# Column copies on VectorE, zeros from ScalarE, and one scaled table a step in a fused transformer and state-space kernel

## The chip, the cores and the metric

The kernel runs as one program on one core of a Trainium2 chip. The metric is the time on the device in microseconds (us), the median of three runs. TensorE is called PE here, VectorE DVE, ScalarE ACT, GpSimd POOL, and SyncE, which issues all the DMAs, SP. "L390" is line 390 of the kernel before.

## What is computed

The input is x, 2048 tokens of 128 features, and everything is in float32. The reference does three things in a row:

```
x = x + 0.5 * ffn(layernorm(x))
x = x + mamba(layernorm(x))
x = x + 0.5 * ffn(layernorm(x))          # the same weights again

def ffn(x):                              # 6 layers
    for i in range(6):
        x = attn_layer(shift_tokens(x), ...) + x
        x = ff_layer(shift_tokens(x), ...) + x
    return x

def shift_tokens(t):                     # the second half of the features is moved by one token
    a, s = split(t, 2, -1)
    return concatenate([a, pad(s, one token in front)[:, :-1]], -1)
```

An attention layer has 16 heads of 64 features. Queries and keys are normalised to length one, multiplied by learned scales and rotated with tables of cosines and sines that depend on the token (`q * cos * scale + rotate_half(q) * sin * scale`). Attention is local: each window of 32 tokens looks at itself and at the window before it; before the first window there is nothing. A feed-forward layer is a layer normalisation, a matmul to twice 341 features, a product of one half with the gelu of the other, and a matmul back. `mamba` is a selective state-space layer with 256 inner features and 16 states, a scan over all 2048 tokens.

## The kernel before

**Tiles and stages.** Features lie on the partitions, tokens in the columns. The 2048 tokens are two segments of 1024 (`SEG`), each eight tiles of 128 (`ST` = 8). The work on one tile in one layer is cut into some 50 stages. A stream of 192 tiles runs through them: the first pass takes segment 0 through its six layers, then segment 1 through its six, and the second pass (`again`) does the same once more. So tile `g` has a segment, a layer and a place `t` from 0 to 7, and 24 stretches of eight tiles follow each other. Stages that work on 256 tokens (the feed-forward ones, and the loading of tables) run once for two tiles, a pair.

**Order.** Nothing is left to a scheduler on PE, DVE, ACT and POOL: the table `ORDER` gives each stage a lag in tiles and a position within a step. In step `i`, `run` calls the stages in the order of their positions, each for tile `i - lag`, and every engine works through its own instructions in that order. So work of up to eight tiles is in flight. Work that belongs to no tile (merging weights, the state-space layer between the passes, the loading of tables for a pair) is put among the stages with `at_time(step + position, ...)`. The order of the DMAs on SP is chosen by the framework from the same program; each is issued when what it waits for is done, and those behind it wait.

**The parts that the change touches.**

The shift by one token is made by storing: a result's second half of partitions is written one column further to the right (`halves`). The residual streams `r0` (one for each segment) and `r1` therefore have 1025 columns, and column 0 of partitions 64 to 127 is what came before the segment: zero for segment 0, and for segment 1 the last column of segment 0 in the same layer. Those last columns are kept in `c0` and `c1`, one column a layer. POOL copies them: L377 and L784 put the last column of `r0` into `c0` (L784 after the feed-forward residual L772 of the pair that ends segment 0), L655 puts that of `r1` into `c1`. POOL also puts them back: L1205 copies `c0` into column 0 of `r0` just before the first projection (`project`, L390) of a layer in segment 1, and L647 copies `c1` into `r1`. In segment 0, L649 sets that column of `r1` to zero on POOL. The state-space layer writes `r0` anew between the passes (`entered`, L375).

Keys and inputs of the window before a tile come from the tile before it (L494, L599). At the head of segment 0 there are none, and POOL writes zeros: L502 into 256 columns of the keys `kt`, L603 into 32 partitions of the inputs `xw`.

The rotation uses tables of cosines and sines multiplied by the layer's learned scales. `tables(p)` makes them for pair `p`. In segment 0 of the first pass it loads the plain table (L292), POOL multiplies it by the scales (L293), it is used, and it is also saved in DRAM for the second pass (L296). At the same place the table of the tokens 1024 further on, which segment 1 will need, is loaded, multiplied and saved. Later, tables are loaded ready (L302). `tables` is called at the stage `TB`, position 0.898 of every odd step, for the next pair; for the first pair it is called at time -1.95, after all weights that the start needs have been issued by `begin`.

On the way of one tile, the lines that the following sections name are: project (L390, two for queries and keys), sines and cosines on DVE (L416, L409), squares on ACT (L402), their sum on DVE (L432), the rotation's addition on POOL (L426), a floor under the sums on POOL (L439), roots on ACT (L444), the copy of the inputs on ACT (L593), the scaling on POOL (L458), scores, maxima, subtraction on POOL (L553), exponent on ACT (L559), divisors on DVE (L564, L565), division on POOL (L569), the average over the window on PE (z_ps, L614), its copy on ACT (L626), mixing by merged value and output weights on PE (L635), the residual on DVE (L651). Merged weights are made at the start (L249, L256) and stored in DRAM (L258).

Of the kernel before, what the change touches and what calls it, by code (L numbers as in the profile page):

```python
# [9 lines left out]
F32 = mybir.dt.float32  # L10
# [7 lines left out]
P = 128  # L18
N = 2048
NB = N // 512  # L20
DEPTH = 6
# [3 lines left out]
WIN = 32  # L25
# [31 lines left out]
ST = 8  # L57
SEG = ST * P
# [59 lines left out]
def halves(at, n):  # L118


    return tuple((rows, bass.ds(at + shift, n)) for rows, shift in SIDES)


class Stream:
# [158 lines left out]
    def tables(self, p):  # L283


        nc, k, st = self.nc, self.k, self.at[2 * p]
        flat = "p a b d -> p (a b d)"

        def scaled(tok, tag, bufs):
            tab = self.sb.tile([P, 4, 2, DH], F32, tag=tag, name="tab", bufs=bufs)  # L290
            at = tok // P % 4
            nc.sync.dma_start(out=tab, in_=k.tabs[:, tok // 512, :, at : at + 2, :])  # L292
            nc.gpsimd.tensor_tensor(  # L293
                tab, tab, st.w.sc.unsqueeze(2).to_broadcast([P, 4, 2, DH]), ALU.mult
            )
            nc.sync.dma_start(out=k.scaled_tabs[st.layer][tok // SUB], in_=tab.rearrange(flat))  # L296
            return tab

        if st.again or st.seg:
            self.tabs[p] = self.sb.tile([P, 4, 2, DH], F32, tag="tab", name="tab")  # L300
            saved = k.scaled_tabs[st.layer][st.tok // SUB]
            nc.sync.dma_start(out=self.tabs[p].rearrange(flat), in_=saved)  # L302
        else:
            self.tabs[p] = scaled(st.tok, "tab", 2)
            scaled(st.tok + SEG, "tab2", 1)

    def next_tables(self, f):
        if f + 1 < len(self.ff):
# [64 lines left out]
    def entered(self, seg, col, xc, q):  # L373
        for rows, cols in halves(col, SUB):
            self.nc.gpsimd.tensor_tensor(self.r0[seg][rows, cols], xc[rows], q[rows], ALU.mult)  # L375
        if seg == 0 and col + SUB == SEG:
            self.nc.gpsimd.tensor_copy(self.c0[64:, 0:1], self.r0[0][64:, SEG : SEG + 1])  # L377

# [108 lines left out]
    def keys_before(self, g):  # L489


        nc, k, st = self.nc, self.k, self.at[g]
        if st.t:
            nc.scalar.activation(  # L494
                st.kt[:, :, 0:WIN], self.at[g - 1].kt[:, :, P:], AF.Identity, scale=k.ratio
            )
        elif st.seg:
            last = self.sb.tile([P, 8, WIN], F32, tag="last", name="last", bufs=1)
            nc.sync.dma_start(out=last.rearrange("p c k -> p (c k)"), in_=k.last_keys[st.layer])
            nc.scalar.copy(st.kt[:, :, 0:WIN], last)  # L500
        else:
            nc.gpsimd.memset(st.kt[:, :, 0:WIN], 0.0)  # L502
        if st.seg == 0 and st.t == ST - 1:
            last = self.sb.tile([P, 8, WIN], F32, tag="last", name="last", bufs=1)
            nc.scalar.activation(last, st.kt[:, :, P:], AF.Identity, scale=k.ratio)
            nc.sync.dma_start(out=k.last_keys[st.layer], in_=last.rearrange("p c k -> p (c k)"))
# [88 lines left out]
    def inputs_before(self, g):  # L595
        nc, k, st = self.nc, self.k, self.at[g]
        nc.sync.dma_start(out=st.xw[WIN:, 0], in_=st.xw[0 : P - WIN, 1])
        if st.t:
            nc.sync.dma_start(out=st.xw[0:WIN, 0], in_=self.at[g - 1].xw[P - WIN :, 1])  # L599
        elif st.seg:  # L600
            nc.sync.dma_start(out=st.xw[0:WIN, 0], in_=k.last_inputs[st.layer])
        else:
            nc.gpsimd.memset(st.xw[0:WIN, 0], 0.0)  # L603
        if st.seg == 0 and st.t == ST - 1:
            nc.sync.dma_start(out=k.last_inputs[st.layer], in_=st.xw[P - WIN :, 1])

# [36 lines left out]
    def residual(self, g):  # L643
        nc, st = self.nc, self.at[g]
        if st.t == 0:
            if st.seg:
                nc.gpsimd.tensor_copy(self.r1[64:, 0:1], self.c1[64:, st.layer : st.layer + 1])  # L647
            else:
                nc.gpsimd.memset(self.r1[64:, 0:1], 0.0)  # L649
        for rows, cols in halves(st.t * P, P):  # L650
            nc.vector.tensor_tensor(  # L651
                self.r1[rows, cols], st.y_ps[rows, :], self.r0[st.seg][rows, cols], ALU.add
            )
        if st.seg == 0 and st.t == ST - 1:
            nc.gpsimd.tensor_copy(  # L655
                self.c1[64:, st.layer : st.layer + 1], self.r1[64:, SEG : SEG + 1]
            )

# [107 lines left out]
    def ff_residual(self, f):  # L766

        nc, st, o = self.nc, self.first(f), self.ff[f].o_ps
        i = V_B2 + st.layer
        for rows, cols in halves(st.t * P, SUB):  # L770
            done = st.layer == DEPTH - 1
            nc.vector.scalar_tensor_tensor(  # L772
                o[rows] if done else self.r0[st.seg][rows, cols],
                o[rows],
                self.k.pv[rows, i : i + 1],
                self.r1[rows, cols],
                ALU.add,
                ALU.add,
            )
            if done:  # L780
                x = self.x[rows, bass.ds(st.tok, SUB)]
                nc.vector.scalar_tensor_tensor(x, o[rows], 0.5, x, ALU.mult, ALU.add)
        if st.seg == 0 and st.t == ST - 2 and st.layer < DEPTH - 1:
            nc.gpsimd.tensor_copy(  # L784
                self.c0[64:, st.layer + 1 : st.layer + 2], self.r0[0][64:, SEG : SEG + 1]
            )

# [343 lines left out]
    def begin(self, x, tp):  # L1131

        nc, k = self.nc, self.k
        self.tp, self.vo = tp, {}
        xi = tp.tile([P, N // P, P], F32, tag="xi", name="xi")

        def read(b):
            nc.sync.dma_start(
                out=xi[:, 4 * b : 4 * b + 4, :],
                in_=x[bass.ts(b, 512), :].rearrange("(t p) d -> p t d", p=P),  # L1140
            )

        def turn(b):
            t_ps = self.bank2(("t_ps", b), 1)[:, 0]
            for j in range(4):
                nc.tensor.transpose(t_ps[:, bass.ts(j, P)], xi[:, 4 * b + j, :], k.ident)
            nc.scalar.copy(self.x[:, bass.ts(b, 512)], t_ps)
            self.used("t_ps", b)

        activation_tables(nc, EXP_LN)  # L1150
        read(0)
        self.load(0)
        read(1)
        self.load_vo(0)
        self.load_ff(0)
        self.load_vo(1)
        read(2)
        read(3)
        for r in (*self.r0, self.r1):
            nc.gpsimd.memset(r[64:, 0:1], 0.0)  # L1160
        at = self.at_time
        at(-2.0, turn, 0)
        at(-1.95, self.tables, 0)
        time = self.enter(0, -1.9, self.sb)
        at(-1.0, turn, 1)
        for s in range(1, 4):
            time = self.enter(s, max(time + 0.1, 2 * s - 2.9), self.sb)
        at(6.5, turn, 2)
        at(8.5, turn, 3)
        for layer in range(DEPTH):  # L1170
            at(layer + 0.6, self.merge, layer)
            if layer == 0:
                at(0.65, self.load_m, 0)
            if layer + 2 < DEPTH:
                at(layer + 0.7, self.load_vo, layer + 2)
            at(self.room(8 * layer + 3.0, 0.1), self.biases, layer)
        for u in range(1, 2 * UNITS):
            at(8 * u - 6.9, self.load, u)
            at(8 * u - 2.9, self.load_m, u)
            at(8 * u - 0.6, self.load_ff, u)  # L1180
# [17 lines left out]
    def stage(self, i, name, lag):  # L1198
        g = i - lag
        if not 0 <= g < TILES:  # L1200
            return
        elif name in self.TILE:
            if name == "PQ" and g % ST == 0 and self.at[g].seg:
                layer = self.at[g].layer
                self.nc.gpsimd.tensor_copy(self.r0[1][64:, 0:1], self.c0[64:, layer : layer + 1])  # L1205
            method, *args = self.TILE[name]
            getattr(self, method)(g, *args)
        elif g % 2:
            getattr(self, self.PAIR[name])(g // 2)
            if name == "YR" and self.at[g].again and self.at[g].layer == DEPTH - 1:  # L1210
                self.at_time(self.room(i + 1.1, 0.1), self.result, g // 2)
# [3 lines left out]
def macaron_kernel(  # L1215
# [18 lines left out]
    nc = tc.nc  # L1234
    k = Ctx()
# [5 lines left out]
    const = ctx.enter_context(tc.tile_pool(name="const", bufs=1))  # L1241
# [23 lines left out]
    nc.vector.memset(k.eps, LN_EPS)  # L1265
    k.minus_one = const.tile([P, 1], F32, tag="minus_one", name="minus_one")
    nc.vector.memset(k.minus_one, -1.0)
    xt = const.tile([P, N], F32, tag="xt", name="xt")

    dram = ctx.enter_context(tc.tile_pool(name="dram", bufs=1, space=bass.MemoryType.DRAM))  # L1270
# [120 lines left out]
```

## Time and profile before

| | |
|---|---|
| median of 3 runs | 3393.36 us (3391.44 to 3393.8) |
| profiled execution | 3395.29 us, span 3393.5 us |
| granted PE clock, mean | 0.993 |
| PE busy (matmuls) | 3231.5 us, 95% |
| DVE busy | 2797.4 us, 82% |
| ACT busy | 2550.1 us, 75% |
| POOL busy | 2925.4 us, 86% |
| DMA | 181.28 MB, mean 53 GB/s |

The span is what the profiler saw from the first instruction to the last; the execution's own time is 1.8 us longer. Busy time is summed over instructions; waiting, branching and the issuing of DMAs are not counted. A matmul's end is modelled, so that a busy PE need not be at its peak. In a row of the timeline the first number is the start, the second the time, then the engine, the line, the operation, what is written and read (out<-in), the shape, and in brackets how long the engine was idle before it and what ended this.

The lines that the change moves are short: a column copy on POOL takes 183 to 188 ns, the memset of `kt` 305 to 333 ns, of `xw` 195 to 197, of `r1` 99 to 100. A multiply of a table (L293) takes 1262 to 1301 ns, and there are 48.

### The profile page before, as it was taken

To read this page: it belongs to the slowest core of one execution; us is meant where nothing else is said; L and a number is where in the kernel's file an instruction comes from. 1 tells how busy PE (TensorE), PEld (TensorE's weight loads), DVE (VectorE), ACT (ScalarE), POOL (GpSimd) and SP (SyncE) were. 2 spreads that over 40 slices of the span, in tenths; PEclk is the share of its full clock that TensorE was granted. 3 is DMA by queue.
4 is the path that set the end of the run, shared out by engine and by line. 5 is a ranking of instruction groups with operands and counts; after the bars stand their busy time and mean duration, and the time that the engine had idled before them with its cause. 6 is when DMAs were issued, how large, how long until landed. Compare 5 with 4: busy or idle time off the path is not lost. (4 is left out here: it accounts for less than half of the span.)

```text
span 3393.5 us, 97541 instructions
## 1 busy us (share of the span) xinstructions
PE 3231.5 (95%) x41936; PEld 2232.1 (66%) x41936; DVE 2797.4 (82%) x3483; ACT 2550.1 (75%) x4097; POOL 2925.4 (86%) x2397
## 2 busy tenths in 40 slices
PE   5999999999999999999999999999999999999997
PEld 3666666666666666666666666666666676777775
DVE  4777788788888898988989888888888788888884
ACT  4777777777778778787787777877877677777775
POOL 5989899898888988889889898888888888888883
PEclk9999999999999999999999999999999999999999
DMA  7211212111112121111111112112121110111000
GB/s 241 93 62 49 74 54 65 65 61 43 57 44 64 38 55 51 52 49 51 55 39 56 49 44 63 45 44 55 46 55 38 49 33 29 46 36 41 19 12 9
DMA packets 134496, 181.28 MB, mean 53 GB/s; under 512 B 13176, under 2 KB 91312, under 8 KB 127152
## 3 DMA queue, kind: packets, MB, share of 16 engines
q1 hardware_dynamic: 134064, 175.04, 17.4%
q8 instruction: 330, 5.41, 0.7%
q14 instruction: 102, 0.84, 0.1%
HBM read 138.75 MB, written 24.05 MB: 48 GB/s over the span
## 5 line engine op out<-in xcount | busy, mean ns | idle before, releaser
L426 POOL TENSOR_TENSOR rot<-rot,t 128x1024 f32<-128x1024 f32 x384 | 900.8, 2368 | 8.9 <-DVE t L416 4.5
L390 PE MATMUL x_ps<-qk,r 128*128 128x512 f32 x1536 | 756.1, 615 | 27.3 <-ACT zt L626 10.3
L635 PEld LDWEIGHTS y_ps<-zt,m 128*128 128x128 f32 x6144 | 715.3, 192 | 62.0 <-ACT xc L681 30.6
L458 POOL TENSOR_TENSOR rot<-rot,rn 128x1024 f32<-128x1024 f32 x384 | 722.9, 1904 | 14.4
L635 PE MATMUL y_ps<-zt,m 128*128 128x128 f32 x6144 | 718.5, 275 | 3.9 <-ACT xc L681 2.7
L416 DVE TENSOR_TENSOR t<-x_ps,tab 128x1024 f32<-128x1024 f32 x384 | 467.9, 1218 | 161.6 <-PE i_ps L586 86.9
L402 ACT ACTIVATE sq<-x_ps 128x1024 f32<-128x1024 f32 x384 | 393.7, 1025 | 261.1 <-DVE rot L409 212.5
L390 PEld LDWEIGHTS x_ps<-qk,r 128*128 128x128 f32 x1536 | 272.4, 191 | 361.9 <-issue 233.3
L569 POOL TENSOR_TENSOR pr<-pr,rs 128x1024 f32<-128x1024 f32 x192 | 365.4, 1903 | 165.1 <-DVE rs L565 139.9
L409 DVE TENSOR_TENSOR rot<-x_ps,tab 128x1024 f32<-128x1024 f32 x384 | 467.7, 1218 | 21.5 <-ACT sq L402 21.0
L626 ACT COPY zt<-z_ps 128x1024 f32<-128x1024 f32 x384 | 369.4, 1010 | 152.9 <-PE z_ps L614 152.8
L432 DVE TENSOR_REDUCE ss<-sq 128x16 f32<-128x1024 f32 x384 | 466.6, 1215 | 14.3 <-ACT sq L402 11.5
L614 PE MATMUL z_ps<-pt,xw 32*128 32x512 f32 x3072 | 414.3, 615 | 5.1 <-ACT qt L480 2.9
L553 POOL TENSOR_TENSOR pr<-pr,mx 128x1024 f32<-128x1024 f32 x192 | 365.7, 1905 | 26.9 <-ACT carry L1080 18.6
L471 PE MATMUL t_ps<-cs,rot 128*128 128x128 f32 x3072 | 371.9, 273 | 5.1 <-DVE sc L1090 2.3
L471 PEld LDWEIGHTS t_ps<-cs,rot 128*128 128x128 f32 x3072 | 344.0, 141 | 34.1 <-issue 9.8
L559 ACT ACTIVATE pr<-pr 128x1024 f32<-128x1024 f32 x192 | 203.4, 1059 | 132.3 <-POOL pr L553 131.4
L529 PE MATMUL s_ps<-kt,qt 64*32 64x64 f32 x24576 | 289.0, 227 | 1.6 <-issue 1.6
L529 PEld LDWEIGHTS s_ps<-kt,qt 64*32 64x32 f32 x24576 | 257.3, 106 | 48.5 <-issue 45.8
L614 PEld LDWEIGHTS z_ps<-pt,xw 32*128 32x128 f32 x3072 | 149.9, 184 | 174.4 <-issue 130.4
L546 DVE TENSOR_REDUCE mx<-s_ps 128x16 f32<-128x1024 f32 x192 | 233.5, 1216 | 16.9 <-PE s_ps L529 16.9
L564 DVE TENSOR_REDUCE rs<-pr 128x16 f32<-128x1024 f32 x192 | 233.1, 1214 | 11.5 <-ACT pr L559 8.6
(142 smaller groups left out, 4821.8 us busy)
## 6 DMA issues: line engine op xcount, KB each, us to landing
bc<-bc SPq DMA_DIRECT2D x64, 512.0 KB, 5.6
tab<-tab SPq DMA_DIRECT2D x120, 256.0 KB, 2.7
qk<-in_wqk_dram SPq DMA_DIRECT2D x24, 1024.0 KB, 4.9
m<-m SPq DMA_DIRECT2D x24, 1024.0 KB, 5.0
tab<-in_tabs_dram SPq DMA_DIRECT2D x48, 256.0 KB, 2.8
xw<-xw SPq DMA_DIRECT2D x192, 48.0 KB, 2.8
m<-mst SPq DMA_DIRECT2D x6, 1024.0 KB
w<-w1s SPq DMA_DIRECT2D x18, 341.0 KB, 3.8
```

The source lines that it names most:

```text
L390: nc.tensor.matmul(out=x[:, j], lhsT=self.columns(g), rhs=st.w.qk[:, bass.ds(kind * INNER + j * 512, 512)], start=True, stop=True,)
L402: self.nc.scalar.activation(st.sq[kind], st.x[kind], AF.Square)
L409: self.nc.vector.tensor_tensor(st.rot[kind], st.x[kind], cos, ALU.mult)
L416: self.nc.vector.tensor_tensor(st.t2[kind].rearrange("p h (two c) -> p h two c", two=2), st.x[kind].rearrange("p h (two c) -> p h two c", ...
L426: self.nc.gpsimd.tensor_tensor(st.rot[kind], st.rot[kind], st.t2[kind], ALU.add)
L432: self.nc.vector.tensor_reduce(st.ss[:, kind, :], st.sq[kind], AX.X, ALU.add)
L458: self.nc.gpsimd.tensor_tensor(st.rot[kind], st.rot[kind], st.rn[:, kind, :].unsqueeze(2).to_broadcast([P, HEADS, DH]), ALU.mult,)
L471: self.nc.tensor.transpose(t_ps[:, c, :], flat[:, bass.ts(c, P)], self.k.ident)
L529: nc.tensor.matmul(out=st.s[32 * b : 32 * b + 32, par, c, :], lhsT=st.qt[rows, c, bass.ts(b, WIN)], rhs=st.kt[rows, c, bass.ds(WIN * b, 2 ...
L614: self.nc.tensor.matmul(out=st.z[b // 2][:, b % 2].rearrange("p (h q) -> p h q", q=WIN), lhsT=st.xw[rows, j, :], rhs=st.pt[rows, :, j, :], ...
L626: self.nc.scalar.copy(st.zt[:, 2 * half : 2 * half + 2].rearrange("p b h q -> p b (h q)"), st.z[half])
L635: self.nc.tensor.matmul(out=st.y_ps.rearrange("p (b q) -> p b q", q=WIN), lhsT=st.w.m[:, h // 2, h % 2, :], rhs=st.zt[:, :, h, :], start=( ...
```

## The change

- The column copies of `residual` and `ff_residual` (L647, L655, L784) and the zero of `r1` (L649) run on DVE in place of POOL.
- The copy of `c0` into column 0 of segment 1's `r0` (L1205) leaves `stage`. For the layers after the first, DVE does it in `residual`, behind the residual of the layer before at `t` = 0. For the first layer of a pass POOL does it in `entered`, when the first block of segment 1 is written.
- The zeros of `kt` and `xw` at the head of segment 0 are copied by ACT from a new constant column `zero`.
- `tables(0)` is called in `begin` right behind `load(0)`, so that its load stands in front of the second block of x and its multiply is POOL's first work.
- The second table of each pair, the one for segment 1, is made at step 2p + 0.9, one step after the first.

PE's instructions and their order stay the same.

```diff
         else:
             self.tabs[p] = scaled(st.tok, "tab", 2)
-            scaled(st.tok + SEG, "tab2", 1)
+            self.at_time(2 * p + 0.9, scaled, st.tok + SEG, "tab2", 1)
...
             self.nc.gpsimd.tensor_copy(self.c0[64:, 0:1], self.r0[0][64:, SEG : SEG + 1])
+        if seg and col == 0:
+            self.nc.gpsimd.tensor_copy(self.r0[1][64:, 0:1], self.c0[64:, 0:1])
...
-            nc.gpsimd.memset(st.kt[:, :, 0:WIN], 0.0)
+            nc.scalar.copy(st.kt[:, :, 0:WIN], k.zero.unsqueeze(2).to_broadcast([P, 8, WIN]))
...
-            nc.gpsimd.memset(st.xw[0:WIN, 0], 0.0)
+            nc.scalar.copy(st.xw[0:WIN, 0], k.zero[0:WIN].to_broadcast([WIN, P]))
...
             if st.seg:
-                nc.gpsimd.tensor_copy(self.r1[64:, 0:1], self.c1[64:, st.layer : st.layer + 1])
+                nc.vector.tensor_copy(self.r1[64:, 0:1], self.c1[64:, st.layer : st.layer + 1])
             else:
-                nc.gpsimd.memset(self.r1[64:, 0:1], 0.0)
+                nc.vector.memset(self.r1[64:, 0:1], 0.0)
...
+        if st.seg and st.t == 0 and st.layer + 1 < DEPTH:
+            nc.vector.tensor_copy(
+                self.r0[1][64:, 0:1], self.c0[64:, st.layer + 1 : st.layer + 2]
+            )
         if st.seg == 0 and st.t == ST - 1:
-            nc.gpsimd.tensor_copy(
+            nc.vector.tensor_copy(
                 self.c1[64:, st.layer : st.layer + 1], self.r1[64:, SEG : SEG + 1]
...
         if st.seg == 0 and st.t == ST - 2 and st.layer < DEPTH - 1:
-            nc.gpsimd.tensor_copy(
+            nc.vector.tensor_copy(
                 self.c0[64:, st.layer + 1 : st.layer + 2], self.r0[0][64:, SEG : SEG + 1]
...
         read(0)
         self.load(0)
+        self.tables(0)
         read(1)
...
-        at(-1.95, self.tables, 0)
...
-            if name == "PQ" and g % ST == 0 and self.at[g].seg:
-                layer = self.at[g].layer
-                self.nc.gpsimd.tensor_copy(self.r0[1][64:, 0:1], self.c0[64:, layer : layer + 1])
```

More of the change, by code (lines that the diff above doesn't have):

```diff
@@ L1267, in macaron_kernel @@
     nc.vector.memset(k.minus_one, -1.0)
+    k.zero = const.tile([P, 1], F32, tag="zero", name="zero")
+    nc.vector.memset(k.zero, 0.0)
     xt = const.tile([P, N], F32, tag="xt", name="xt")
```

## The prediction

> **What bounds the kernel now.** I read the page's busy times first, then two stretches of equal work, then who waited for whom, then the timeline at two places.
>
> ```profile
> PE 3231.5 (95%) x41936; PEld 2232.1 (66%) x41936; DVE 2797.4 (82%) x3483; ACT 2550.1 (75%) x4097; POOL 2925.4 (86%) x2397
> ```
>
> ```profile
> 470.00:599.00 129.00, 126.94 (x1728) 89.25 (x1727) 103.16 (x127) 95.27 (x146) 118.72 (x98) 1.00 0.20 64
> ...
> 2874.00:2997.00 123.00, 123.00 (x1714) 87.23 (x1712) 102.84 (x125) 94.33 (x145) 108.42 (x87) 1.00 0.12 37
> ```
>
> The first line is the page's; the two of the second fence are one layer's eight tiles each (columns: window, its length, then busy time of PE, PE's weight load, DVE, ACT, POOL, granted clock, DMA). At 2874 PE is busy in all 123.0 us: with nothing else wrong, PE sets the time. At 470, in the first half sequence, the same work takes 129.0. Some 1.7 of the difference are bias matmuls; the rest is PE waiting. So only what takes PE's waits away shortens the kernel, and the question for each edit is which wait of PE hangs on it.
>
> ```profile
> POOL c L784 <- DVE r L772: 51.3, 10, 8.0
> ...
> PEld x_ps L390 <- POOL r L1205: 11.7, 6, 2.8
> ```
>
> These are waits in total, their number and the longest. The first does not name PE, but POOL runs its queue in order, and the timeline shows who is behind it:
>
> ```profile
> 2234.77 0.18 POOL L784 COPY c<-r 64x1 f32<-64x1 f32 x1 [4.55 <-DVE r L772]
> ...
> 2241.29 0.28 POOL L439 TENSOR_SCALAR ss<-ss 128x32 f32<-128x32 f32 x1
> ...
> 2241.61 0.23 ACT L444 ACTIVATE y<-ss 128x32 f32<-128x32 f32 x1 [3.98 <-POOL ss L439]
> ...
> 2242.57 0.70 PE L670 MATMUL c_ps<-r,cs 128*128 128x256 f32 x2 [2.80 <-ACT xw L593]
> ```
>
> A copy of one column held POOL for 4.55 us, so the floor (L439) came late behind two L426, ACT stood before its logarithm with the copy L593 behind it, and PE waited 2.80 us for a PSUM bank.
>
> **The change, part by part.**
>
> *Column copies L784 (10) and L655 (12) from POOL to DVE.* On DVE they follow the instruction that makes their data, so POOL's wait goes. What PE loses after each L784, read from the timeline as the wait within some 20 us plus what the next z_ps group (L614) takes above its usual 2.00 us: in the second pass 2.93 at 1946 (with about 1.7 more, below), 1.69+1.36 at 2093, 2.80+1.36 at 2243, 1.55 at 2388, 1.69+1.36 at 2534, together 16.4. In the first pass 1.5 at 252 and at 389 (1.2 of z_ps, 0.3 more wait than beside other column-free steps), 1.84+1.36 at 527, 1.76+1.36 at 656, 2.01+1.11 at 785, together 12.4. Sum **28.8 us**. L655 idles POOL 15.0 us in 8 places, but no PE wait follows: nothing.
>
> *Column copy L1205 (12) from POOL, just before x_ps, to DVE, behind the residual three to four steps (some 50 us) earlier.* It has no wait of its own (0.1 us of idle); it is late because POOL's long multiplies stand before it. PE waits 0.93, 2.00, 0.59, 0.42, 2.01 and 1.22 us at six of the twelve.
>
> ```profile
> 1103.36 0.19 POOL L1205 COPY r<-c 64x1 f32<-64x1 f32 x1
> ...
> 1103.60 3.40 PE L390 MATMUL x_ps<-qk,r 128*128 128x512 f32 x4 [2.00 <-POOL r L1205]
> ```
>
> ```profile
> 1104.10:1107.40 3.30, 3.30 (x7) 1.01 (x5) 0.31 (x1) 0.27 (x2) 3.05 (x5) 0.50 0.00 0
> ```
>
> Two of them cost more than their wait: behind 2.00 us of idle the granted clock is 0.50 for 3.4 us, and the four matmuls take 3.40 instead of 1.98; at 1540 they take 3.20. [...] The row decides: 7.2 of waits and 2.6 of slow clock, **9.8 us**.
>
> *What DVE and ACT get.* DVE: 22 + 22 column copies, 12 one-column memsets. Nearest rows: 146 ns for 128x1 (L1263), 59 ns for a 128x1 memset: 7 us over the kernel, while DVE idles 20 us in every layer stretch, so nothing. Without that cover it would be 7. Behind them on DVE stand L564 and L565, for which POOL's L569 waits (139.9 us in 70 places): 0.15 us later each, covered by POOL's own arrears. [...] The trace holds no DVE copy beside a busy POOL; the nearest row is
>
> ```profile
> L565 DVE RECIPROCAL rs<-rs x192: 252/253/255, 69.8 to 3354.5; 128x16 f32<-128x16 f32 x192
> ```
>
> one source, SBUF to SBUF, never stretched in 192 cases. I take 0 and keep 19 for the range.
> ACT: 12 zero copies of 128x256 (418 ns, L500) and 12 of 32x128 (at most L593's 248 ns): 8 us. The first stands where other tiles run L494 (520 ns), the second before L402, where ACT waits for DVE anyway (212.5 us in 158 places): nothing. POOL loses 12 x (323+195+99) ns of memsets.
>
> *One scaled table a step.* Two L293 (1.28 us each) stood together at the end of each odd step; now the second follows a step later. In the first half sequence z_ps runs 1.94 us long at 100, and 0.96, 0.96, 0.96, 0.90, 0.86 at 233, 370, 502, 630, 759, because ACT's exponent waits for POOL's L553, which stands behind the pair. 1.28 us less in front of it covers these: **6.6 us**. The next step's floor stands behind the same total as before, so no new arrears. Each table still is one load and one save on SP; they are now spread too, and a load has two steps (30 us) until POOL needs it, against a landing of 2.8.
>
> *First tables behind the first weights.*
>
> ```profile
> 23.05 2.48 POOL L293 TENSOR_TENSOR tab<-tab,sc 128x512 f32<-128x512 f32 x2 [22.17 <-DMA tab<-in_tabs_dram]
> ...
> 35.00 2.36 POOL L426 TENSOR_TENSOR rot<-rot,t 128x1024 f32<-128x1024 f32 x1 [1.80 <-DVE rot L409]
> ...
> 37.82 0.34 SPq L258 DMA_DIRECT2D m<-mst  x1
> ```
>
> POOL waits 22.2 us for the tables, issued at 18.27, with L375 behind it until 25.49, though that one's q is ready at 12.8. The new load takes the second x block's place in the queue (that one landed at 13.2), pushing it back by 256 KB, about 1.2 us. Then L293 ends at 14.5, L375 at 16.3; the second block gives its xc at about 17.6 and x_ps starts at 19.4 instead of 28.94, 9.5 us sooner. But the program's order puts a trap behind it: on SP the second table's load now stands behind the store of the first merged matrix (L258), which waits for ACT, and on POOL its multiply stands before the first L426. Moved 9.5 us, the store goes out at 28.3, wo and the table at 28.7 and 29.2; with 1.8 MB at the 350 GB/s of the stretch 36 to 42 and 1.8 us of start, the table lands at about 35.5, POOL is free at 36.8, later than the 35.00 of before. The two L426 then run back to back to 41.5; the floor that ran at 43.97 is sooner by **2.4 us**. Landing at 32 gives 5.8, at 38 nothing; these are the ends. The save of the first table also holds SP until 14.5, covered by wv in the DMA queue until about 16.6.
>
> **Sum.** 28.8 + 9.8 + 6.6 + 2.4 = 47.6. Not all will be kept: in steps without these waits PE still shows 0.2 to 0.6 us for ACT's zt or xw copies at the same places, so I leave 0.35 at each of 16 places, 5.6 us, and take 42. The profiled execution took 3395.3 with its span of 3393.5; the median of the runs is 3393.4, so 42 off the median: **3351 us**.
>
> **Rivals.** (1) *The waits are handed on* (0.24): without L784 POOL next waits at L569 for DVE's L565, which comes after the same L772. For it: L569's 139.9 us. Against: the floor L439 stands before L569, and ACT and PE hang on the floor. If half of 47.6 stays lost, 3370. (2) *The start costs* (0.08): the second table lands at 43, POOL's first L426 at 44.3, 5 us lost in place of 2.4 won: 3359. (3) *Slower*: DVE's copies block behind GpSimd's multiplies (0.12), each at the place where L564 or the next residual follows. [...] (4) The main case, 0.56.
>
> **Numbers.** The main case spans 3338 (47.6 whole, 3.4 more at the start, and PE's wait of 2.83 for xw at 72 with its slow clock) to 3364 (rival 1 in a quarter of the sum); rival 1 reaches 3378, and rival 3 at 0.9 us a copy with half of it reaching PE gives 3370. Range 3336 to 3380. A change of 0.2%, 6.8 us, is about what can be told from none; rival 3 puts 0.09 above it and 0.03 inside, all else is faster: 0.88.
>
> **What would show it.** Right: no POOL wait for L772 before a column copy; ACT's wait for L439 and PE's for xw much shorter behind it; layer stretches of the first half near 125; no x_ps wait at the segments' start and two or three half-clock stretches fewer; x_ps at 19 to 20 with POOL waiting for a table near 30 to 36. Wrong: DVE column copies far above 0.2 us; PE waits of the same size with another name; or the first L426 after 38.

## The result, and the profile after

| | before | after |
|---|---|---|
| median, first measurement | 3393.58 us (4 runs, 3391.44 to 3397.03) | 3353.24 us (4 runs, 3351.7 to 3355.14) |
| ratio | | 0.9880, 95% interval 0.9863 to 0.9898 |
| median, second measurement, another chip | 3396.09 us (14 runs, 3392.21 to 3399.23) | 3352.34 us (4 runs, 3352.18 to 3353.3) |
| ratio | | 0.9877, 95% interval 0.9863 to 0.9890 |
| profiled execution, span | 3395.29 us, 3393.5 us | 3351.7 us, 3349.9 us |

The changed kernel is 40.3 us faster in the first measurement and 43.8 in the second; 42 were forecast, 3351 us. In the middle of its file the lines stand 2 further down than before, in the second half 6: x_ps is L392, POOL's addition L428, the floor L441, ACT's first root L446, POOL's subtraction L555, the divisors L566 and L567, the division L571, z_ps L616, the column copy L784 now L790.

Busy times, from the page:

```profile
PE 3214.8 (96%) x41936; PEld 2229.3 (67%) x41936; DVE 2803.8 (84%) x3540; ACT 2554.2 (76%) x4121; POOL 2909.8 (87%) x2317
```

The same two stretches of eight tiles as before (window, its length, busy PE, PE's weight load, DVE, ACT, POOL, granted clock, DMA):

```profile
465.20:590.00 124.80, 124.80 (x1731) 88.54 (x1730) 103.41 (x131) 95.69 (x148) 117.85 (x93) 1.00 0.21 66
2828.00:2951.00 123.00, 123.00 (x1716) 87.28 (x1720) 103.14 (x128) 94.36 (x145) 108.02 (x85) 1.00 0.13 37
```

The stretch that took 129.0 us takes 124.8, and PE has no idle left in it. The stretch that was full before is as long as before. What was won is time that PE lost to others, not work: the number of matmuls is the same. Only part of it shows as idle time. In the first stretch 2.06 us of idle went and 2.14 us of busy time (126.94 to 124.80); over the whole span PE's idle fell by 26.9 us and its busy time by 16.7. Of these 16.7 us 11.6 are in z_ps, whose groups ran long while they waited inside (414.3 us at L614, now 402.7), and 5.1 in x_ps, 2.6 of these at 1103.60 and 1540.29, where it ran at a granted clock of 0.50.

Who waited for whom (total us, times, longest us):

```profile
POOL pr L571 <- DVE rs L567: 171.9, 86, 8.1
...
ACT y L446 <- POOL ss L441: 22.0, 7, 13.0
```

and before:

```profile
POOL pr L569 <- DVE rs L565: 139.9, 70, 8.5
...
ACT y L444 <- POOL ss L439: 43.7, 25, 5.2
```

The column copy's wait of 51.3 us is gone. ACT waits for the floor 7 times instead of 25, and 22.0 us instead of 43.7; 13.0 of the 22.0 are one wait at the start. POOL's wait for the reciprocal grew from 139.9 to 171.9: it was handed on there. The timeline at the place of the second pass that was shown before tells why that does no harm:

```profile
2198.16 0.15 DVE L790 COPY c<-r 64x1 f32<-64x1 f32 x1
...
2199.91 0.28 POOL L441 TENSOR_SCALAR ss<-ss 128x32 f32<-128x32 f32 x1
2200.16 1.90 POOL L571 TENSOR_TENSOR pr<-pr,rs 128x1024 f32<-128x1024 f32 x1
...
2201.20 0.23 ACT L446 ACTIVATE y<-ss 128x32 f32<-128x32 f32 x1
...
2201.86 0.25 ACT L595 COPY xw<-i_ps 128x128 f32<-128x128 f32 x1
...
2203.44 0.70 PE L676 MATMUL c_ps<-r,cs 128*128 128x256 f32 x2
```

The floor runs 1.75 us after the copy; before it was 6.52. ACT comes to its logarithm without standing idle, its copy L595 follows, and c_ps has no wait; before, it had 2.80. The wait for L567 is that of L571, and L571 stands behind the floor in POOL's queue.

At the place of the projection that had waited 2.00 us and then ran at half clock for 3.40 (before: 1103.60):

```profile
1079.82 2.00 PE L616 MATMUL z_ps<-pt,xw 32*128 32x512 f32 x16
...
1081.75 1.98 PE L392 MATMUL x_ps<-qk,r 128*128 128x512 f32 x4
```

No wait, and 1.98 us. Not every wait at such a place was the copy's: at 1245 and 2563 (before) the one that came last was ACT's copy of z_ps, and there PE still waits. The first of the two, before and after:

```profile
1245.25 1.95 PE L390 MATMUL x_ps<-qk,r 128*128 128x512 f32 x4 [0.62 <-ACT zt L626]
```

```profile
1221.92 1.98 PE L392 MATMUL x_ps<-qk,r 128*128 128x512 f32 x4 [0.53 <-ACT zt L628]
```

And the copies on DVE and the zeros on ACT, by line (number, shortest, median and longest in ns):

```profile
L790 DVE COPY c<-r x10: 150/150/151, 247.8 to 2484.5; 64x1 f32<-64x1 f32 x10
...
L657 DVE COPY r<-c x10: 143/144/145, 878.5 to 3103.7; 64x1 f32<-64x1 f32 x10
...
L649 DVE COPY r<-c x12: 150/150/152, 877.8 to 3226.0; 64x1 f32<-64x1 f32 x12
...
L661 DVE COPY c<-r x12: 150/150/152, 212.4 to 2585.4; 64x1 f32<-64x1 f32 x12
...
L605 ACT COPY xw<-zero x12: 279/291/293, 55.4 to 2417.7; 32x128 f32<-32x128 f32 x12
```

At the start, POOL's queue (in brackets the idle time and what ended it):

```profile
33.64 1.26 POOL L293 TENSOR_TENSOR tab<-tab,sc 128x512 f32<-128x512 f32 x1 [12.17 <-DMA tab<-in_tabs_dram]
34.86 4.65 POOL L428 TENSOR_TENSOR rot<-rot,t 128x1024 f32<-128x1024 f32 x2
39.60 0.28 POOL L441 TENSOR_SCALAR ss<-ss 128x32 f32<-128x32 f32 x1
```

Before, the floor ran 4.4 us later:

```profile
43.97 0.29 POOL L439 TENSOR_SCALAR ss<-ss 128x32 f32<-128x32 f32 x1
```

And SP's queue, in which the second table's load follows the store of the first merged matrix:

```profile
25.67 0.34 SPq L258 DMA_DIRECT2D m<-mst  x1
26.07 0.43 SPq L236 DMA_DIRECT2D wo<-in_wo_dram  x1
26.55 1.17 SPq L292 DMA_DIRECT2D tab<-in_tabs_dram  x1
```

### The profile page after: what moved, and what is told of

Read it like the earlier page. It is cut to its first block, busy times and chain, and to the rows that moved or that the text cites. A ratio compares the mean times of both kernels' runs of the same rounds, so it can differ in the third digit from the quotient of the medians.

```text
span 3349.9 us, 97482 instructions
## 1 busy us (share of the span) xinstructions
PE 3214.8 (96%) x41936; PEld 2229.3 (67%) x41936; DVE 2803.8 (84%) x3540; ACT 2554.2 (76%) x4121; POOL 2909.8 (87%) x2317
## 4 chain that ended last, share of the span: by engine, by line
PE 68%; DVE 12%; ACT 10%; POOL 7%; issue 2%; DMA 0%; SPq 0%; POOLq 0%; DVEq 0%; ACTq 0%
PE x_ps L392 16%; PE y_ps L637 15%; PE z_ps L616 8%; PE t_ps L473 7%; PE s_ps L531 6%; PE g_ps L718 3%; PE o_ps L764 3%; PE a_ps L718 3%; DVE da L1075 2%; DVE rot L411 2%; POOL rot L460 2%; DVE t L418 2%; PE y_ps L1109 1%; ACT da L1064 1%; PE s_ps L520 1%
## 5 line engine op out<-in xcount | busy, mean ns | idle before, releaser
L428 POOL TENSOR_TENSOR rot<-rot,t 128x1024 f32<-128x1024 f32 x384 | 901.0, 2369 | 2.9 <-DVE t L418 2.7
L392 PE MATMUL x_ps<-qk,r 128*128 128x512 f32 x1536 | 751.0, 611 | 22.0 <-ACT zt L628 10.1
L571 POOL TENSOR_TENSOR pr<-pr,rs 128x1024 f32<-128x1024 f32 x192 | 365.5, 1904 | 202.4 <-DVE rs L567 171.9
L392 PEld LDWEIGHTS x_ps<-qk,r 128*128 128x128 f32 x1536 | 270.9, 190 | 356.5 <-issue 235.3
L616 PE MATMUL z_ps<-pt,xw 32*128 32x512 f32 x3072 | 402.7, 614 | 3.0 <-DVE t L418 1.4
L555 POOL TENSOR_TENSOR pr<-pr,mx 128x1024 f32<-128x1024 f32 x192 | 365.7, 1905 | 27.3 <-ACT carry L1086 19.3
L616 PEld LDWEIGHTS z_ps<-pt,xw 32*128 32x128 f32 x3072 | 147.4, 184 | 163.3 <-issue 130.3
L482 ACT COPY qt<-t_ps 128x1024 f32<-128x1024 f32 x192 | 193.9, 1010 | 60.3 <-PE t_ps L473 56.3
```

What stands on the lines that cost most here:

```text
L392: nc.tensor.matmul(out=x[:, j], lhsT=self.columns(g), rhs=st.w.qk[:, bass.ds(kind * INNER + j * 512, 512)], start=True, stop=True,)
L428: self.nc.gpsimd.tensor_tensor(st.rot[kind], st.rot[kind], st.t2[kind], ALU.add)
L616: self.nc.tensor.matmul(out=st.z[b // 2][:, b % 2].rearrange("p (h q) -> p h q", q=WIN), lhsT=st.xw[rows, j, :], rhs=st.pt[rows, :, j, :], ...
```

## The experiments

Times are medians; ratios are to the kernel before on the same chip in the same measurement, whose median lay at 3396.04, 3396.09 or 3396.66 us. What is undone in the changed kernel, or added to it, is held against its second measurement, 3352.34 us; only two of these runs (tables together, small rest) were on the same chip as that, so a difference of a few us between the others and it is weak by itself, and the traces are read beside it. A gain "by trace" is the difference in the start of a stage that runs once a tile (L564 before, L566 after), read at the first tile of each layer.

**The c0 column alone on DVE.**

```diff
         if st.seg == 0 and st.t == ST - 2 and st.layer < DEPTH - 1:
-            nc.gpsimd.tensor_copy(
+            nc.vector.tensor_copy(
                 self.c0[64:, st.layer + 1 : st.layer + 2], self.r0[0][64:, SEG : SEG + 1]
```

> The kernel before with one part of the change alone: the column copy of L784 (10 of them) goes from POOL to DVE. Theory (POOL's wait for L772 makes the floor late, and what PE loses behind it is won whole): 28.8 us less than before, 3365 us (3361 to 3369), with the line for POOL's c at L784 gone from the waits. Rival 1 (half of it is handed on to POOL's next wait, L569): 3379. A third reading (the first pass owes its gain to the split tables, which the change brought at the same steps, and the copy is worth only its second pass): about 16.5 less, 3377.

Measured: 3363.71 us (3362.09 to 3366.12), 32.3 less than before, ratio 0.9902 (0.9886 to 0.9919). Ten copies of one column make three quarters of the gain. By trace, the five steps of the second pass give 15.3 us (the prediction's working had 16.4), and one of the half-clock stretches of before among them is still there (2384.0, here 2359.2); in the trace of the next experiment, where it is gone, they give 16.9. The first pass gives 9.0 (12.4): the places at 252 and 389, put down at 1.5 us each, gave 0.1 and 0.2. Most of those 1.5 us was a z_ps group, which this kernel has as well (3.17 us), and the changed one too. Before and in the changed kernel:

```profile
269.84 3.18 PE L614 MATMUL z_ps<-pt,xw 32*128 32x512 f32 x16
```

```profile
265.27 3.19 PE L616 MATMUL z_ps<-pt,xw 32*128 32x512 f32 x16
```

Another 3.7 us lie between the passes' steps and 1.5 behind the last of them, where nothing was edited: there the trace of before has four half-clock stretches (at 1104.0, 1503.4, 1540.9 and 2660.5), this one only one (1707.3). With 0.9 at the start and 1.2 lost in the tail this makes the 29.2 by which the span is shorter.

**The same copy, still on POOL, but behind the floor.**

```diff
+        st = self.first(f)
+        if st.seg == 0 and st.t == ST - 2 and st.layer < DEPTH - 1:
+            self.at_time(2 * f + 8.3, self.keep_column, st.layer + 1)
+
+    def keep_column(self, layer):
+        self.nc.gpsimd.tensor_copy(
+            self.c0[64:, layer : layer + 1], self.r0[0][64:, SEG : SEG + 1]
+        )
...
-        if st.seg == 0 and st.t == ST - 2 and st.layer < DEPTH - 1:
-            nc.gpsimd.tensor_copy(
-                self.c0[64:, st.layer + 1 : st.layer + 2], self.r0[0][64:, SEG : SEG + 1]
-            )
```

> The kernel before, in which the copy of L784 stays on POOL, but is issued in the next step, behind the floor L439; nothing else moves. Theory (what costs is the place in POOL's queue, in front of the floor, and not the engine or the 0.18 us of the copy): as much as on DVE within 2 us, 3365 to 3369. Rival (POOL is simply overloaded and any instruction taken from it helps): the ten copies are still there, 0.18 us each, so at most 2 us are won and it stays at 3391 to 3394.

Measured: 3364.02 us (3362.33 to 3367.72), ratio 0.9906 (0.9892 to 0.9921), the same as on DVE. The row of the moved copy, and what POOL waited for before it:

```profile
L731 POOL COPY c<-r x10: 182/182/183, 253.3 to 2500.0; 64x1 f32<-64x1 f32 x10
its engine sat idle before it (us, times) until:
  DVE r L780: 7.2, 4
```

The copy takes its 182 ns on POOL as before, ten times, and POOL even waits 7.2 us for it. That costs PE nothing, since the floor stands ahead of it. What was won is the order in POOL's queue: POOL's load is the same as before.

**The r0 column put back on POOL, in the changed kernel.**

```diff
-        if seg and col == 0:
-            self.nc.gpsimd.tensor_copy(self.r0[1][64:, 0:1], self.c0[64:, 0:1])
...
-        if st.seg and st.t == 0 and st.layer + 1 < DEPTH:
-            nc.vector.tensor_copy(
-                self.r0[1][64:, 0:1], self.c0[64:, st.layer + 1 : st.layer + 2]
-            )
...
+            if name == "PQ" and g % ST == 0 and self.at[g].seg:
+                layer = self.at[g].layer
+                self.nc.gpsimd.tensor_copy(self.r0[1][64:, 0:1], self.c0[64:, layer : layer + 1])
```

> The changed kernel with one part undone: the column of r0 is again copied by POOL just before x_ps (L1205 of before). Theory (7.2 us of waits of PE and 2.6 us of half clock behind two of them): 9.8 us more than the changed kernel, 3363 (3360 to 3366), with x_ps waiting for POOL again in about six places and two or three more half-clock stretches. [...] Rival (the waits at x_ps are taken up later in the step): 3353 to 3356.

Measured: 3355.92 us (3355.2 to 3357.95), ratio to before 0.9882 (0.9867 to 0.9897). That is 3.6 more than the changed kernel (other chip, other runs; the intervals of the two ratios overlap), where 9.8 had been expected. The waits are back: who waited (PE's weight load, PEld, and PE itself), and the timeline in the third layer of the first pass, with its granted clock (the third number from the end of the window's row):

```profile
PEld x_ps L390 <- POOL r L1205: 11.6, 6, 2.8
...
PE x_ps L390 <- POOL r L1205: 5.3, 4, 2.0
```

```profile
1084.74 1.98 PE L390 MATMUL x_ps<-qk,r 128*128 128x512 f32 x4 [1.97 <-POOL r L1205]
```

```profile
1084.70:1088.00 3.30, 3.26 (x101) 1.83 (x104) 1.18 (x2) 0.89 (x5) 2.98 (x5) 1.00 0.00 0
```

The line of PEld is that of before (11.7, 6 times), and so is PE's own, which was

```profile
PE x_ps L390 <- POOL r L1205: 5.4, 4, 2.0
```

So the copy makes PE wait in four places, not six, and for 5.4 us, not 7.2: the other 1.8 us are the two waits for ACT's copy of z_ps shown above. And behind 1.97 us of idle the clock is 1.00 and x_ps takes 1.98 us, where before, behind 2.00 us, it was 0.50 and 3.40. The same holds in the sixth layer (1517.8: wait 1.99, x_ps 1.98), which had 3.20 before. So the 2.6 us of slow clock don't go with these waits in every execution. By trace this part costs some 5.6 us in the first pass (5.5 and 5.7 against the two profiles of the changed kernel), which is the four waits; the time shows 3.6.

**The r0 column alone, in the kernel before.** The edit is the reverse of the last one.

> The kernel before with the column of r0 alone (L1205) moved to DVE behind the residual. Prediction's step (7.2 us of waits and 2.6 of half clock): 9.8 us less than before, 0.29%. After the run that undid this part in the changed kernel, whose trace has the same 5.3 us of PE's waits in four places but normal clock behind 2.0 us of idle in two of them: 5 to 6 us less, 0.16%. Rival (the wait is taken up later, because POOL's floor is late in these steps anyway while L784 stays): 0 to 2 us less.

Measured: 3387.43 us (10 runs, 3383.66 to 3392.41), 8.7 less than before, ratio 0.9977 (0.9968 to 0.9986). That is near the 9.8 of the prediction and above the 5 to 6 of the second guess, which the interval (4.8 to 10.9 us) doesn't exclude. The rival, that L784 would take the gain back (0 to 2 us), is out.

**The tables of a pair together again.**

```diff
-            self.at_time(2 * p + 0.9, scaled, st.tok + SEG, "tab2", 1)
+            if p:
+                scaled(st.tok + SEG, "tab2", 1)
+            else:
+                self.at_time(0.9, scaled, st.tok + SEG, "tab2", 1)
```

> The changed kernel with the two tables of a step scaled together again, as before, except for the first pair, which stays apart. Theory (z_ps waits for L553 behind the pair, 1.94 and five times some 0.9 us): 6.6 us more than the changed kernel, less what the first pair keeps (1.94), so 4.7 more, 0.14% (3 to 6.6). Rival (the pair was only late because the column copies held POOL before it; without them POOL takes the 1.28 us in its stride): 0 to 1.5 us more.

Measured: 3351.86 us (3351.32 to 3354.85), ratio 0.9877 (0.9862 to 0.9892): nothing. The five z_ps groups that had run 0.9 us long take 2.00. The sixth is back at 3.94 (at 95.9; the changed kernel has 2.73), so it hangs on the second pair, which is scaled together here, and not on the first; the whole time does not show it.

**The small rest back on POOL.**

```diff
-            nc.scalar.copy(st.kt[:, :, 0:WIN], k.zero.unsqueeze(2).to_broadcast([P, 8, WIN]))
+            nc.gpsimd.memset(st.kt[:, :, 0:WIN], 0.0)
...
-            nc.scalar.copy(st.xw[0:WIN, 0], k.zero[0:WIN].to_broadcast([WIN, P]))
+            nc.gpsimd.memset(st.xw[0:WIN, 0], 0.0)
...
-                nc.vector.tensor_copy(self.r1[64:, 0:1], self.c1[64:, st.layer : st.layer + 1])
+                nc.gpsimd.tensor_copy(self.r1[64:, 0:1], self.c1[64:, st.layer : st.layer + 1])
...
-                nc.vector.memset(self.r1[64:, 0:1], 0.0)
+                nc.gpsimd.memset(self.r1[64:, 0:1], 0.0)
...
-            nc.vector.tensor_copy(
+            nc.gpsimd.tensor_copy(
                 self.c1[64:, st.layer : st.layer + 1], self.r1[64:, SEG : SEG + 1]
```

> The changed kernel with the small rest put back on POOL: the c1 column copies (L655, L647 of before), the r1 zero, and the zeros of kt and xw. Only the c0 and r0 columns and the tables stay changed. Theory (no wait of PE hangs on these): 0 us, within 2 of the changed kernel, though POOL again waits some 15 us for L651 before its L655. Rival A (12 times 0.6 us of memsets stand in front of POOL's work for PE): 3 to 7 us more. Rival B (L655 makes the floor late as L784 did): 8 to 15 us more.

Measured: 3350.26 us (3349.72 to 3357.16), ratio 0.9875 (0.9861 to 0.9888): nothing.

**Tables and rest together.** Both of the last two edits in one kernel.

> The changed kernel with two parts undone together that cost nothing when undone one at a time: the tables of a pair scaled together (all but the first) and the c1 columns and zeros back on POOL. Theory (the 6.6 us of the tables are there, but either 1.28 us of table or 0.6 us of memsets taken from POOL's queue is enough to bring L553 back in time, so that each alone shows nothing): z_ps is again 0.9 long once a layer from the third on, 4 to 6 us more than the changed kernel, 3356 to 3358. Rival (tables and rest are worth nothing, and the 4 us by which the c0 copy alone fell short of the whole in the first half sequence belong to another part): 0 to 1.5 us more.

Measured: 3358.98 us (3356.7 to 3362.09), ratio 0.9890 (0.9877 to 0.9904): 6.6 more than the changed kernel and a little above the 4 to 6 expected. Two parts that cost nothing one at a time cost 6.6 us together. POOL's subtraction and z_ps in this kernel, at the place that was long at 233 before:

```profile
226.62 1.90 POOL L558 TENSOR_TENSOR pr<-pr,mx 128x1024 f32<-128x1024 f32 x1
...
228.56 1.06 ACT L564 ACTIVATE pr<-pr 128x1024 f32<-128x1024 f32 x1 [2.60 <-POOL pr L558]
...
229.63 2.92 PE L619 MATMUL z_ps<-pt,xw 32*128 32x512 f32 x16
...
230.57 0.31 PEld L619 LDWEIGHTS z_ps<-pt,xw 32*128 32x128 f32 x8 [0.64 <-ACT qt L485]
```

and in the one with the tables together, but the rest off POOL:

```profile
229.33 2.00 PE L619 MATMUL z_ps<-pt,xw 32*128 32x512 f32 x16
```

With both undone, z_ps takes 2.92 or 2.93 once in each layer from the second on (at 229.6, 365.9, 497.4, 627.1 and 752.6), and 3.94 at 96.2: 5.8 us in all. The subtraction is late, ACT's exponent with it, and ACT's copies of queries and keys behind that, of which z_ps waits for the first (the last row). Taking either part out of POOL's queue, the 1.28 us of table or the small rest, brings those five z_ps back to 2.00. Which piece of the rest does it, its 0.6 us of memsets or its column copies, was not tried.

**The first tables loaded late again.**

```diff
         self.load(0)
-        self.tables(0)
         read(1)
...
+        at(-1.95, self.tables, 0)
```

> The changed kernel, but the first tables are loaded where before had them, behind the fourth x block; the second of the pair still comes a step later, and all else stays changed. Prediction's step: what the earlier load wins at the floor, 2.4 (0 to 5.8) more, by the trace of the changed kernel 3.4 more, 0.10%: 3355. Rival (as in the run with the second table's load moved ahead, where the floor came 7 us sooner and the next step gave it back, the start hangs on the loads and stores of the second step): within 1.5 us of the changed kernel.

Measured: 3356.1 us (3353.23 to 3358.48), ratio 0.9881 (0.9867 to 0.9894): 3.8 more than the changed kernel, on another chip; the intervals overlap. By trace the first layer is reached 0.6 us sooner than before, against 3.4 and 3.8 in the two profiles of the changed kernel, so this part is worth some 3 us there.

**The second table's load taken from behind the store.**

```diff
-            self.at_time(2 * p + 0.9, scaled, st.tok + SEG, "tab2", 1)
+            second = st.tok + SEG
+            if p:
+                self.at_time(2 * p + 0.9, lambda: scale(load(second, "tab2", 1), second))
+            else:
+                self.load_second = lambda: load(second, "tab2", 1)
+                self.at_time(0.9, lambda: scale(self.tab2, second))
...
         read(1)
+        self.tab2 = self.load_second()
```

`load` and `scale` are the two halves of `scaled`.

> The changed kernel, but the second table of the first pair is loaded behind the first x blocks, so that only its multiply and its save stay at time 0.9; its load no longer stands behind the store of the first merged matrix. Theory (POOL's wait of 12.2 us at L293 until 33.64 is what keeps the start's gain at 3.4 us): L293 no longer waits, POOL's first L428 starts near 24 instead of 34.86, the floor is about 5 to 8 us sooner, and the time is about 3348 (3343 to 3350). Rival (the start hangs on something else too, such as the merged matrix, its store and ACT's queue): L428 is sooner, but PE's u0 ends where it did, 3352 to 3354.

Measured: 3350.44 us (3349.14 to 3351.74), ratio 0.9865 (0.9850 to 0.9880): some 2 us less than the changed kernel, between the theory's range and the rival's. By trace nothing was won at the start, as the rival had it: the first layer is reached 0.8 us sooner than before, against 3.4 and 3.8. POOL's queue in this kernel (its lines: L296 the table, L436 the addition, L449 the floor):

```profile
23.93 2.35 POOL L436 TENSOR_TENSOR rot<-rot,t 128x1024 f32<-128x1024 f32 x1 [0.46 <-DVE rot L419]
...
32.96 0.28 POOL L449 TENSOR_SCALAR ss<-ss 128x32 f32<-128x32 f32 x1
...
49.85 1.26 POOL L296 TENSOR_TENSOR tab<-tab,sc 128x512 f32<-128x512 f32 x1 [10.95 <-DMA tab<-in_tabs_dram]
51.07 4.65 POOL L436 TENSOR_TENSOR rot<-rot,t 128x1024 f32<-128x1024 f32 x2
55.80 0.28 POOL L449 TENSOR_SCALAR ss<-ss 128x32 f32<-128x32 f32 x1
```

SP's queue and PE:

```profile
39.94 0.33 SPq L258 DMA_DIRECT2D m<-mst  x1
...
41.98 3.16 SPq L292 DMA_DIRECT2D tab<-in_tabs_dram  x1
```

```profile
58.18 2.08 PE L249 MATMUL m_ps<-wo,wv 64*128 64x128 f32 x16 [8.61 <-ACT sq L412]
```

The first step did as it should: the addition starts at 23.93 instead of 34.86, the floor runs at 32.96 instead of 39.60. Then POOL waits 10.95 us for the next table, whose load (41.98) stands behind the store of the *second* merged matrix (39.94), and PE waits 8.61 us at 58.18. The trap was there twice.

**Both loads taken from behind the stores.** The last kernel, and the first table of the second pair is loaded behind the fourth x block:

```diff
+            self.tabs[p] = self.early.pop(p, None) or load(st.tok, "tab", 2)
...
         read(3)
+        self.early[1] = self.load_next()
```

> The changed kernel, in which the second table of the first pair and the first table of the second pair are both loaded with the first x blocks, so that neither load stands behind a store of a merged matrix; multiplies and saves stay where they were. Theory (in the run that moved only the first of these loads, POOL waited 10.9 us for the other until 49.85, the floor came at 55.80 and PE then waited 8.61 us at 58.18): that wait of POOL goes, the floor comes before 50 and PE's 8.61 with it: 5 to 8 us less than the changed kernel, 3345 (3343 to 3348), ratio 0.9855. Rival (the wait moves on to the next load, store or merge, a step later): 3350 to 3352.

Measured: 3342.53 us (5 runs, 3341.76 to 3343.74), ratio 0.9841 (0.9827 to 0.9854): 54 us less than before and 9.8 less than the changed kernel (another chip), more than the 5 to 8 expected. In its trace (the table is L296, the addition L437, the floor L450):

```profile
38.29 1.27 POOL L296 TENSOR_TENSOR tab<-tab,sc 128x512 f32<-128x512 f32 x1
39.51 2.39 POOL L437 TENSOR_TENSOR rot<-rot,t 128x1024 f32<-128x1024 f32 x1
...
46.19 0.28 POOL L450 TENSOR_SCALAR ss<-ss 128x32 f32<-128x32 f32 x1
```

```profile
49.34 1.16 PE L249 MATMUL m_ps<-wo,wv 64*128 64x128 f32 x16 [0.32 <-ACT sq L413]
```

POOL doesn't wait for this table, the floor of the second step runs at 46.19 instead of 55.80, and PE waits 0.32 us in place of 8.61. By trace the first layer is reached 11.5 us sooner than before (3.4 to 3.8 in the changed kernel), and this stays to the end. The first load alone won some 2 us, both together 9.8; the second alone was not tried. The order of SP's queue held a gain that POOL, DVE and PE were ready for.

**The changed kernel again.**

> The changed kernel itself, beside the parts of it on the same chip, so that parts and whole stand against the same runs of before. Expected 0.988 of before (0.9865 to 0.9895), as in the first measurement.

Measured: 3352.34 us, ratio 0.9877, as in the table at the top.

## Why the prediction was right, point by point

The time lay 2.2 us from the forecast in the first measurement, and the main case was right in what makes most of the gain: the column copy in front of the floor. That the total came so near is in part luck, since the parts did not all come out by their own numbers and their errors went both ways:

| part | predicted | alone | undone in the changed kernel |
|---|---|---|---|
| c0 column (L784) | 28.8 | 32.3 | |
| r0 column (L1205) | 9.8 | 8.7 | 3.6 |
| one table a step | 6.6 | | 0; with the rest 6.6 |
| small rest (L655, L647, zeros) | 0 | | 0; with the tables 6.6 |
| first tables | 2.4 | | 3.8 |
| all | 42 (47.6 less 5.6) | 40.3 and 43.8 | |

- **L784: right in mechanism, by the engine's order.** The copy behind the floor on POOL, as fast as the one on DVE, shows that it is the place in the queue. The second pass was 15.3 and 16.9 in two traces (16.4). The first was read too high: 9.0 for 12.4, most of it because at 252 and 389 a long z_ps, 1.2 us each, was put down to the copy; it is still there in the changed kernel. The about 1.7 more at 1946, part of the 16.4, is the half clock there: 0.50 from 1947.12 to 1950.51, where s_ps took 2.05 us and y_ps 2.59; at full clock groups of the same form took 1.52 and 1.98 (1087.09 and 1088.54 with the r0 column put back). "L655 idles POOL 15.0 us, but no PE wait follows: nothing" held.
- **L1205: four waits of six right, the slow clock wrong as a rule.** Of the 7.2 us of waits 5.4 were the copy's, and these came back when it was undone (5.6 by trace). The 0.59 and 1.22 at 1245 and 2563 end on ACT's copy of z_ps and stayed. The 2.6 us of half clock were counted as part of two waits. They fell there in that one execution: behind the same waits of 1.97 to 1.99 us, two other traces (the copy put back; the c0 column alone) have a full clock. The 8.7 measured alone lies near 9.8, but its interval, 4.8 to 10.9, holds 5.4 as well.
- **Tables: the sum right, the owner wrong.** The step "1.28 us less in front of it covers these: 6.6 us" holds only as long as the small rest is on POOL. That was taken off too, and costed at nothing. Either of the two edits wins the whole of it where the other is missing, and adds nothing where the other is made. In the changed kernel the z_ps at 100 fell from 3.94 to 2.73, not to 2.00; the other five to 2.00.
- **Start: the trap right, a size off.** The second table's load did stand behind the store, and its multiply before the first addition. All came sooner than worked out: x_ps at 17.21 (19.4), the load's issue at 26.55 (29.2), POOL free at 34.86 (36.8), so 3.4 to 3.8 us in place of 2.4. That the trap stands at the second merged matrix once more was not seen. Until the first was removed it did not show.
- **"Not all will be kept", 5.6 us: the total right, the reason not shown.** In the first profile of the changed kernel 46.3 of the 47.6 us were there when the last four layers began, in the second 43.5; half-clock stretches at 323.1, 1695.3 and 2128.8 stand in the second alone. In the first the tail gave 2.7 back, with one more such stretch at 3310.1. New waits for the zt or xw copies don't explain it: over the whole span PE's idle before them fell (xw 42.1 to 36.1 us, zt 13.2 to 10.4).
- **Rival 1, the waits handed on:** they were (139.9 to 171.9 us at L571), and PE did not pay for it, as the argument against it said: the floor stands in front.
- **Rival 2, the start costs:** L428 began before 38, at 34.86.
- **Rival 3, DVE's copies block:** no run shows the 0.9 us a copy, nor the 19 us that stand for it in the range. In the changed kernel all 44 column copies took 143 to 152 ns, beside a POOL that is busy 87%; none was held up. The flat row of L565 (252 to 255 ns) was the right sign, though it is no copy.
- **ACT:** the zeros of `xw` take 291 ns, above the bound of 248; behind them two weight loads waited 0.5 us together.

## What to carry to other kernels

On an engine that works in order, a short instruction that waits costs what stands behind it (here a copy of 0.18 us that waited 4.55, and the floor 6.52 us behind the copy's start): look for the place in the queue where nothing urgent follows before changing the engine. Where two edits relieve the same late instruction, undo them together as well as one at a time, or both look worthless. When a load is moved ahead and the gain does not come, read the issue queue for the next load that stands behind the same kind of store.

## What the runs showed of the hardware

**The clock.** Between 80 us after the start and 90 us before the end the profile of before has six half-clock stretches, at 1104.02, 1503.38, 1540.92, 1947.11, 2384.01 and 2660.49, and the first profile of the changed kernel has one, at 2613.80. Each is 3.41 us long, and those of before begin whole multiples of 3.413 us apart. That part of both profiles was divided into cells of this length, in step with the stretches, and these were sorted by how long PE idled in them:

| PE idle within one cell | cells | followed by a cell at half clock |
|---|---|---|
| 2.1 us or more | 3 | 3 |
| 1.85 to 2.1 | 3 | 2 |
| 1.5 to 1.85 | 21 | 2 |
| 1.0 to 1.5 | 42 | 0 |
| less than 1.0 | 1806 | 0 |

Two cells of before, each with the one that follows it (window, its length, busy PE; the clock is the third number from the end):

```profile
1100.61:1104.01 3.40, 1.40 (x13) 0.46 (x6) 1.55 (x3) 2.31 (x5) 3.17 (x4) 1.00 0.02 5
1104.03:1107.42 3.39, 3.39 (x7) 1.01 (x5) 0.33 (x1) 0.36 (x2) 3.14 (x5) 0.50 0.00 0
...
2240.65:2244.05 3.40, 1.49 (x5) 0.96 (x6) 1.44 (x2) 2.38 (x7) 3.14 (x6) 1.00 0.43 76
2244.07:2247.40 3.33, 3.33 (x27) 2.85 (x26) 3.10 (x4) 1.88 (x3) 3.25 (x3) 1.00 0.00 0
```

The first holds the wait for L1205: 2.00 us of idle, and the next cell ran at 0.50. In the second PE idled 1.91 us, and the next ran at 1.00. With the copy put back the clock was 1.00 behind a wait of 1.97 us (1084.74), and with the c0 column alone on DVE behind one of 1.99 us (1093.32). So a wait of about 2 us was followed by half clock in some places and not in others; what decides was not shown. Which waits are hit changes from one execution to the next: when the last four layers began, two profiles of the changed kernel (mean clock 0.994 and 0.992) stood 2.8 us apart, with three half-clock stretches in the one that the other lacks. That is more than the effect of some of the change's parts.

**Short copies.** A copy of 64x1 took 143 to 152 ns on DVE and 182 to 188 ns on POOL, and a zero of 64x1 59 ns on DVE and 99 to 100 ns on POOL. What the ten at L784 cost in place, with PE waiting behind them, was some 3 us each (32.3 us for the ten).
